# Which engines follow a hand-written table of times in a four-layer graph network: all five, or TensorE, VectorE and SyncE's queue alone

## The chip, the cores and the metric

The kernel runs on one core of one Trainium2 chip. The metric is device time in microseconds from the first to the last instruction of the program on that core; smaller is better. A core has five instruction streams that run side by side and wait for each other through semaphores: TensorE (PE, matrix products), VectorE (DVE), ScalarE (ACT), GpSimd (POOL) and SyncE (SP), which here only issues DMAs. Each stream runs strictly in its own order: an instruction that waits holds up everything behind it on its engine.

## The reference

64 independent graphs of 256 nodes with 512 features go through four layers. Each layer normalizes `x`, applies ReLU, runs a graph layer on the result and adds it to `x`. Cut to what matters:

```python
def _layernorm(x): return (x - mean) / sqrt(var + 1e-5)       # over the 512 features

# layer 0: q, k = split(h @ W_qk.T);  w = softmax(sum(q k^T / 8 * adj, -1), over nodes);  out = w * (h @ W_v.T)
# layer 1 (8 heads of 64):
feats = einsum('bnf,hfu->bhnu', X, W)
dense = leaky_relu(e_self[..., :, None] + e_neigh[..., None, :], 0.2)
dense = dense + NEG_BIG * (1.0 - A[:, None, :, :])
att = softmax(dense, axis=-1)
out = relu(einsum('bhij,bhju->bhiu', att, feats) + b)
# layer 2: Xp = X Wp + bp; attn = tanh(A * (Xp C^T) Xp^T) per head; out = relu(attn Xp)
# layer 3: q, k = split(h @ Wqk); w = sum(q * (adj @ (k * mask))) / sqrt(512); out = softmax(w) * (h @ Wv)
for each layer:
    h = maximum(_layernorm(x), 0)
    x = x + layer(h, adj)
```

## The kernel before

For each graph `b` the kernel defines some 150 small *steps* (a normalization, a product, a DMA). A table gives each step a time within its graph; a new graph starts every `PERIOD`, so five graphs are in work at once, each in another layer. The steps of all graphs are recorded in the order of these times. A scheduler then orders each engine's stream, but an engine in `PINNED` gets an edge from each of its instructions to the one recorded before it, so its stream is exactly the order of the table.

```python
PINNED = (mybir.EngineType.PE, mybir.EngineType.Activation, mybir.EngineType.DVE, mybir.EngineType.Pool, mybir.EngineType.SP,)

PERIOD = 60.2
TIMES = { ...
    "max2": 74.244, "ea1": 75.256, "max0": 75.757, "max3": 76.069, "ea3": 77.200, "ea0": 78.017, "max1": 78.219,
    "mxv": 78.317, "ea2": 80.651, "eg2": 82.397, "mxt": 85.102, "eg0": 86.489, "mr": 87.558, "eg1": 88.075, ...
    "eg3": 96.405, ...
    "yr": 197.444, "yv": 199.505, "yg": 201.580, "st3": 202.086, "rs3": 203.471, "pw3": 205.848, ... }
...
    def run(self, weights, graph, count):
        for _, b, name in self.sequence(count):
            ...
            graphs[b].steps[name]()
            for i in traced[n:]:
                if i.engine in PINNED:
                    if i.engine in self.last:
                        self.tc.add_manual_dep(i, self.last[i.engine], ... NoSync ..., reason="plan")
                    self.last[i.engine] = i.name
```

The steps that the text below follows, from three different layers, are these. Layer 1 (attention): `max` finds the largest masked score of each row, on VectorE; `ea`, `eg`, `eb`, `ex` make the attention weights of two heads, on four engines in turn; `po` is the product with the features.

```python
    def largest(i):                                   # max0..3: 16 instructions for a graph
        for h in range(i % 2 * 4, i % 2 * 4 + 4):
            nc.vector.tensor_tensor_reduce(junk, g["en"][:, h, :], g["adj"][:, c, :], 1.0, -BIG,
                                           OP.add, OP.max, g["mx"][:, c, h:h + 1])          # L851
    # mxv: four small VectorE instructions on mx (L861 to L865); mxt: a transpose of mx (L870)
    # mr, mb: DMAs of the result to DRAM and back to all partitions, as m

    def attention(p):                                 # p = 0..3, two heads each
        # ea{p}: four times
        nc.scalar.activation(e[:, s, j, :], g["es"][:, h, :], AF.Prelu, bias=..., alpha=0.2)   # L890
        # eg{p}:
        nc.gpsimd.tensor_tensor(e, e, g["negt"][:, None].to_broadcast([P, 2, NC, N]), OP.add)  # L897
        # eb{p}:
        nc.vector.tensor_tensor(e, e, g["m"][...], OP.subtract)                                # L903
        # ex{p}:
        nc.scalar.activation(g[f"e{p}"], g[f"e{p}"], AF.Exp)                                   # L909
        # po{p}: matmuls of e with feats (L921)
```

The end of layer 2 (`yg` on GpSimd and `yv` on VectorE add the layer's output to the two halves of `x`) and the start of layer 3 (normalization, `L662` to `L685`):

```python
        # yr: DMA sq_d -> hn (y)
        add_output(0, "yg", nc.gpsimd)      # L1076: xt[:, 0] += y[:, 0]
        add_output(1, "yv", nc.vector)      # L1076: xt[:, 1] += y[:, 1]
    # normed(layer): st: bn_stats, bn_aggr (L662, L664) | rs: var + eps (L669, VectorE)
    #   pw: power -0.5 (L673, GpSimd) | sh: -mean * rstd (L678, VectorE)
    #   hn: relu(x * rstd + shift), two halves (L685, ScalarE) | sq: transposes (L617) | sw, ht: DMAs
```

The end of layer 3, for the graph before that one, and the start of layer 0, for the graph after:

```python
    # zv1: row sums of q * aggregate (L1116, VectorE) -> wc
    # softp: TensorE spreads wc (L723) | softv: row maximum (L728, VectorE)
    # softa: exp on ScalarE (L733, L735) | softw, add: L740, L741, L747 on VectorE
    # qk0, qk1: projections on TensorE | qe0, qe1: copies of them to SBUF (L763, ScalarE)
    # score0: matmul that reads qk (L773, TensorE) | agg0, agg1: matmuls that read hn of layer 3 (L1095)
    # ga0, ga1: copies of agg (L1104, ScalarE) | xcv, xca: copies of xc (L995, ScalarE)
```

Of the kernel before, what the change touches and what calls it, by code (L numbers as in the profile page):

```python
# [31 lines left out]
NEG_BIG = -1e10  # L32
BIG = 3.0e38

PINNED = (mybir.EngineType.PE, mybir.EngineType.Activation, mybir.EngineType.DVE, mybir.EngineType.Pool, mybir.EngineType.SP,)

PERIOD = 60.2
TIMES = {
# [308 lines left out]
class Plan:  # L347
# [20 lines left out]
    def run(self, weights, graph, count):  # L368
        graphs = {-1: weights()}
        for _, b, name in self.sequence(count):  # L370
# [5 lines left out]
# [3 lines that stand above are left out]
# [783 lines left out]
```

## Time and profile before

| | |
|---|---|
| time, median of three runs | 3899.43 us (3897.83 to 3902.69) |
| profiled execution, span | 3884.0 us |
| granted TensorE clock, mean | 0.992 |
| ScalarE busy | 1668.5 us (43%) |
| DMA share of 16 engines | 60.8% |
| GpSimd L897 (`eg`), 256 of them | 601.8 us, 2371 ns each |
| GpSimd L1076 (`yg`), 64 of them | 108.2 us, 1691 ns each |
| VectorE L851 (`max`), 1024 of them | 446.3 us, 436 ns each |
| VectorE L678 (`sh`), 256 of them | 158.3 us, 618 ns each |

The span holds 64 graphs. In the middle of the run the same pattern comes back every 58.6 us: the `hn` of one layer starts at 1901.91 us and its successor at 1960.50 us. A span of 58.6 us of the timeline is therefore the unit in which everything below is counted. In a line of the timeline the first number is the start in us, the second the time from the first start to the last end of the merged instructions, then engine, line, operation, output and inputs, the count, and in brackets the idle time before and what ended it.

### The profile page before, as it was taken

How to read it: one execution, taken by the hardware profiler on the slowest of the kernel's cores; microseconds unless marked ns; L12 is line 12 of the kernel's file. 1: busy time of each engine (PE TensorE's matmuls, PEld its weight loads, DVE VectorE, ACT ScalarE, POOL GpSimd, SP SyncE). 2: the span in 40 equal slices, each digit the busy share in tenths (PEclk: the TensorE clock that was granted, in tenths of full speed). 3: DMA queues.
4: the chain of work that ended last, by engine and by line, in shares of the span. 5: the costliest groups of instructions: out<-in, count | busy, mean ns of one | idle time of the engine just before them, and what ended most of it. 6: DMA issues, size and time to landing. Idle time of an engine off the chain costs nothing.

```text
span 3884.0 us, 53839 instructions
## 1 busy us (share of the span) xinstructions
PE 3809.3 (98%) x17218; PEld 2443.6 (63%) x17218; DVE 3025.1 (78%) x7769; ACT 1668.5 (43%) x3205; POOL 1264.8 (33%) x1100
## 2 busy tenths in 40 slices
PE   7999999999999999999999999999999999999989
PEld 4756666666666666666666666666666666665564
DVE  6887888878877877877888778778777778776774
ACT  2443444444444444444444444444444444443342
POOL 1332333333333323323323323323323333333231
PEclk9999999999999999999999999999999999999989
DMA  7565666665665665666666666666666666665543
GB/s 211 177 190 170 188 189 185 192 194 176 199 196 174 200 195 177 197 194 180 193 190 188 191 190 188 188 189 189 187 188 191 186 190 191 185 190 163 173 149 107
DMA packets 921353, 717.64 MB, mean 185 GB/s; under 512 B 783792, under 2 KB 821232, under 8 KB 896496
## 3 DMA queue, kind: packets, MB, share of 16 engines
q1 hardware_dynamic: 921072, 714.21, 60.8%
q8 instruction: 138, 2.26, 0.2%
q14 instruction: 143, 1.17, 0.1%
HBM read 477.56 MB, written 236.45 MB: 184 GB/s over the span
## 4 chain that ended last, share of the span: by engine, by line
PE 88%; DVE 6%; DMA 3%; issue 1%; SPq 1%; ACT 0%; POOL 0%; DVEq 0%; POOLq 0%; ACTq 0%
PE bank L611 55%; PE bank L921 12%; PE bank L1009 6%; PE bank L1023 5%; PE bank L1095 5%; PE bank L987 3%; DVE junk L851 2%; PE bank L773 1%; DMA sq_d<-sq 1%; DVE sq L617 1%; PE bank L723 1%; DMA all<-m_d 1%; DMA all<-er_d 1%; DVE pair L903 1%; DMA ht<-sq_d 1%
## 5 line engine op out<-in xcount | busy, mean ns | idle before, releaser
L611 PE MATMUL bank<-w_s,ht 128*128 128x256 f32 (+2 forms) x3072 | 949.9, 462 | 14.8 <-DMA ht<-sq_d 9.5
L611 PE MATMUL bank<-wv_s,ht 128*128 128x512 f32 x2048 | 916.6, 595 | 0.0
L611 PEld LDWEIGHTS bank<-w_s,ht 128*128 128x128 f32 x3072 | 595.3, 197 | 352.3 <-issue 237.9
L611 PEld LDWEIGHTS bank<-wv_s,ht 128*128 128x128 f32 x2048 | 393.0, 197 | 415.4 <-issue 400.9
L897 POOL TENSOR_TENSOR pair<-pair,negt 128x1024 f32<-128x1024 f32 x256 | 601.8, 2371 | 51.5 <-ACT pair L890 47.3
L685 ACT ACTIVATE hn<-xt,shift,rstd 128x512 f32<-128x512 f32 x512 | 388.8, 806 | 433.1 <-DVE shift L678 424.4
L921 PEld LDWEIGHTS bank<-feats,pair 128*128 128x128 f32 x4096 | 512.2, 200 | 54.3 <-issue 29.6
L1048 ACT ACTIVATE pair<-pair 128x512 f32<-128x512 f32 x512 | 299.2, 625 | 558.4 <-DVE pair L1041 558.1
L921 PE MATMUL bank<-feats,pair 128*128 128x65 f32 x4096 | 507.5, 283 | 17.5 <-ACT pair L909 17.5
L890 ACT ACTIVATE pair<-all,ec 128x256 f32<-128x256 f32 x1024 | 417.1, 494 | 229.6 <-DMA all<-er_d 225.6
L851 DVE CUSTOM_DVE_ANT_0 junk<-all,adj 128x256 f32<-128x256 f32 x1024 | 446.3, 436 | 38.2 <-DMA all<-er_d 4.8
L611 PE MATMUL bank<-m_s,ht 128*128 128x512 f32 x1024 | 466.3, 599 | 1.9 <-DMA ht<-sq_d 1.2
L673 POOL TENSOR_TENSOR rstd<-rstd,power 128x2 f32<-128x2 f32 x256 | 180.2, 704 | 845.7 <-DVE rstd L669 715.7
L1041 DVE TENSOR_TENSOR pair<-bank,at 128x512 f32<-128x512 f32 x512 | 325.8, 679 | 109.6 <-PE bank L1009 108.7
L617 DVE STREAM_TRANSPOSE sq<-hn 128x512 f32<-128x512 f32 x512 | 338.5, 694 | 59.9 <-ACT hn L685 59.7
L1076 POOL TENSOR_TENSOR xt<-xt,hn 128x512 f32<-128x512 f32 x64 | 108.2, 1691 | 840.8 <-DMA hn<-sq_d 712.1
L903 DVE TENSOR_TENSOR pair<-pair,all 128x1024 f32<-128x1024 f32 x256 | 309.8, 1230 | 57.6 <-DMA all<-m_d 53.7
L662 DVE BATCH_NORM_STATS2 stats<-xt 128x6 f32<-128x512 f32 x512 | 327.2, 681 | 34.2 <-POOL xt L1076 27.5
L611 PEld LDWEIGHTS bank<-m_s,ht 128*128 128x128 f32 x1024 | 195.9, 196 | 208.4 <-issue 202.3
L946 POOL TENSOR_TENSOR xt<-xt,o 128x256 f32<-128x256 f32 x256 | 183.8, 728 | 409.1 <-DVE o L938 300.8
L909 ACT ACTIVATE pair<-pair 128x1024 f32<-128x1024 f32 x256 | 262.3, 1047 | 55.3 <-DVE pair L903 49.9
L1009 PE MATMUL bank<-xc,xpt 64*128 64x256 f32 x2048 | 256.7, 390 | 0.9 <-ACT xc L995 0.7
(74 smaller groups left out, 3793.2 us busy)
## 6 DMA issues: line engine op xcount, KB each, us to landing
sq_d<-sq SPq DMA_DIRECT2D x384, 512.0 KB
ht<-sq_d SPq DMA_DIRECT2D x1024, 128.0 KB
all<-er_d SPq DMA_DIRECT2D x128, 1024.0 KB
all<-m_d SPq DMA_DIRECT2D x64, 1024.0 KB
xt<-in_x_dram SPq DMA_DIRECT2D x64, 512.0 KB
xpt<-sq_d SPq DMA_DIRECT2D x256, 128.0 KB
hn<-sq_d SPq DMA_DIRECT2D x256, 128.0 KB
out_dram<-xt SPq DMA_DIRECT2D x64, 512.0 KB
```

Source lines behind the costliest of these rows:

```text
L611: nc.tensor.matmul(p, chunk(ht[:, k], c), w[:, k], start=(k == 0), stop=(k == KC - 1))
L617: nc.vector.transpose(sq.rearrange("p (r k i c) -> p c k r i", r=4, k=KC, c=NC)[:, c], t[:, c])
L662: nc.vector.bn_stats(stats[:, c, :], g["xt"][:, c, :])
L685: nc.scalar.activation(hn[:, c, :], g["xt"][:, c, :], AF.Relu, bias=st["shift"][:, c:c + 1], scale=st["rstd"][:, c:c + 1])
L851: nc.vector.tensor_tensor_reduce(junk, g["en"][:, h, :], g["adj"][:, c, :], 1.0, -BIG, OP.add, OP.max, g["mx"][:, c, h:h + 1])
L890: nc.scalar.activation(e[:, s, j, :], g["es"][:, h, :], AF.Prelu, bias=st["ec"][:, j, H + h:H + h + 1], alpha=0.2)
L897: nc.gpsimd.tensor_tensor(e, e, g["negt"][:, None].to_broadcast([P, 2, NC, N]), OP.add)
L903: nc.vector.tensor_tensor(e, e, g["m"][:, 2 * p:2 * p + 2, None, :].to_broadcast([P, 2, NC, N]), OP.subtract)
L921: nc.tensor.matmul(po[:, h % 4, :], chunk(e[:, s, j], i), feats[:, j, h, :], start=(j == 0), stop=(j == NC - 1))
L1009: nc.tensor.matmul(ps[s][:, m, :], chunk(g["xpt"][half, p], m), g["xc"][half, p, :], start=True, stop=True)
L1041: nc.vector.tensor_tensor(th[:, s], g[f"ps{p}{s}"].rearrange("p (m n) -> p m n", m=NC), g["at"], OP.mult)
L1048: nc.scalar.activation(g[f"th{p}"][:, s], g[f"th{p}"][:, s], AF.Tanh)
```

## The change

ScalarE and GpSimd are taken out of `PINNED`. Their data dependencies stay, and each is then ordered by the scheduler as it judges best; the other three streams stay tied to the table. The purpose is to let the two engines take whatever is ready, instead of standing before a step whose inputs the table expected earlier.

```diff
-PINNED = (mybir.EngineType.PE, mybir.EngineType.Activation, mybir.EngineType.DVE, mybir.EngineType.Pool, mybir.EngineType.SP,)
+PINNED = (mybir.EngineType.PE, mybir.EngineType.DVE, mybir.EngineType.SP,)
```

In the built programs, the streams of TensorE, VectorE and SyncE are the same instructions in the same order, with the same buffers. ScalarE and GpSimd have the same instructions in another order. In the middle of the run, GpSimd's order for one period is

```
before: am am, neg, negt, pw, yg, eg, pw, eg eg eg, pw, pa pa pa pa, pw
after:  neg, am am, negt, pw, eg eg eg eg, yg, pw, pw, pa pa pa pa, pw
```

and ScalarE's, from the copies `ye` on (`hn'` is one half of an `hn`, `softa` and `w` the two exponentials of a softmax):

```
before: ye ye hn, ea ea ea ea, qe qe hn, softa3 w3, softa0 w0, ex, ga0, ex ex, ga1, hn, ex, xcv xca, ta ta hn ta ta
after:  ye ye hn, ea ea ea ea, softa3, qe, hn', qe, hn', w3, ga0, ex, softa0 w0, ex, ga1, ex, xcv, hn, ex, xca, ta ta ta hn ta
```

(`ta`: the tanh of layer 2; neighbours such as `ex` and `ga` change places from one period to the next.)

## The prediction

> **What bounds the kernel now.** I read the page's first and second parts, then the waits of TensorE, then the timeline of one period, and last the same instructions early in the run, where the order of GpSimd was already once what the change makes of it.
>
> From the first part of the page, and from the waits of TensorE:
>
> ```profile
> PE 3809.3 (98%) x17218; PEld 2443.6 (63%) x17218; DVE 3025.1 (78%) x7769; ACT 1668.5 (43%) x3205; POOL 1264.8 (33%) x1100
> ...
> PE bank L921 <- ACT pair L909: 17.5, 7, 5.1
> ...
> PE bank L723 <- DVE bank L1116: 10.4, 4, 4.2
> ```
>
> TensorE is idle for 3884.0 - 3809.3 = 75 us in all. A busy share of pipelined matmuls alone proves little, but here the longest wait of TensorE for anyone adds up to 17.5 us in 7 times, and these lie in the filling and emptying of the pipeline of graphs. In the middle TensorE never waits. Two things follow. There is next to nothing to win: at most those 75 us, 2%, and most of them need the first and last graphs. And every microsecond by which TensorE is made to wait in a period of 58.6 us is paid in full, once for each graph. ScalarE (43%) and GpSimd (33%) have much idle time, so their order matters only through what they do to others.
>
> Now the timeline of one period, from the last `max` instructions to the first matmul of `score0`:
>
> ```profile
> 1918.03 6.49 ACT L890 ACTIVATE pair<-all,ec 128x256 f32<-128x256 f32 x16 [3.46 <-DMA all<-er_d]
> ...
> 1922.21 0.42 DVE L851 CUSTOM_DVE_ANT_0 junk<-all,adj 128x256 f32<-128x256 f32 x1
> ...
> 1923.31 0.17 DVE L865 TENSOR_TENSOR mx<-mx 128x16 f32<-128x16 f32 x1
> ...
> 1925.34 0.69 DVE L1076 TENSOR_TENSOR xt<-xt,hn 128x512 f32<-128x512 f32 x1 [1.86 <-DMA hn<-sq_d]
> 1925.44 1.72 POOL L1076 TENSOR_TENSOR xt<-xt,hn 128x512 f32<-128x512 f32 x1 [13.46 <-DMA hn<-sq_d]
> ...
> 1926.62 0.14 DVE L1116 DVE_READ_ACCUMULATOR bank<-bank,mask_c,cols 128x1 f32 x1
> ...
> 1927.12 2.35 POOL L897 TENSOR_TENSOR pair<-pair,negt 128x1024 f32<-128x1024 f32 x1
> ...
> 1929.06 0.14 PEld L723 LDWEIGHTS bank<-ident,wc 128*128 128x128 f32 x1 [0.23 <-issue]
> ...
> 1930.25 7.02 POOL L897 TENSOR_TENSOR pair<-pair,negt 128x1024 f32<-128x1024 f32 x3
> 1930.41 2.21 DVE L678 SCALAR_TENSOR_TENSOR shift<-mv,rstd 128x2 f32<-128x2 f32 x1
> ```
>
> The reader is to see four things. (1) GpSimd stands idle for 13.46 us before `yg`, while ScalarE has finished the first pair (four of the 16 L890) near 1919.7: the table makes `eg` wait behind `yg`. (2) Meanwhile VectorE runs the 16 `max` instructions undisturbed, 0.42 us each, one every 0.465 us, to 1922.63. (3) `zv1` ends at 1926.76 and TensorE takes its result at 1929.06, so it has 2.3 us to spare; over the steady periods this distance is 1.4 to 2.8 us, mostly 2.4. (4) Once `eg` runs, a VectorE instruction on 128x2 elements (L678) takes 2.21 us and ends when the running `eg` ends; in the 184 cases with no GpSimd instruction beside it the median is 0.15 us.
>
> The timeline of an early graph shows what happens when `eg` and `max` do meet:
>
> ```profile
> 214.99 0.43 DVE L851 CUSTOM_DVE_ANT_0 junk<-all,adj 128x256 f32<-128x256 f32 x1
> 215.02 7.60 POOL L897 TENSOR_TENSOR pair<-pair,negt 128x1024 f32<-128x1024 f32 x3 [5.51 <-ACT pair L890]
> ...
> 215.46 2.46 DVE L851 CUSTOM_DVE_ANT_0 junk<-all,adj 128x256 f32<-128x256 f32 x1
> ...
> 217.96 2.45 DVE L851 CUSTOM_DVE_ANT_0 junk<-all,adj 128x256 f32<-128x256 f32 x1
> ```
>
> They take turns: one `max` for each `eg`, start to start 217.96 - 215.46 = 2.50 us in place of 0.465.
>
> **What the Trainium skill says.** "SBUF — State Buffer", section "Who interferes with whom": a VectorE instruction with two SBUF inputs contends with a GpSimd instruction that reads SBUF, and the one that comes second is blocked for the whole instruction, not slowed. The trace agrees: L851 (`en` and `adj`, both in SBUF) 2.45 us, L678 2.21 us; while L1116, with one tensor in PSUM, has a median of 751 ns with and without GpSimd beside it. "TensorE: Matmul & The Clock Gate", section "Part 1: The HAM clock gate (the "warmup" mystery)": after an idle window of about 3.4 us TensorE's clock is halved, until a busy window has passed. The trace agrees: all idle gaps of TensorE over 3.2 us after its start are followed by a stretch at clock 0.50 of 3.4, 6.8 or 13.7 us, and there the 512-column matmuls start every 853 ns, against 429 ns elsewhere.
>
> **The change, part by part.** VectorE, TensorE and SyncE keep their order, so I move GpSimd's and ScalarE's instructions to the new order and keep every measured duration.
>
> *GpSimd: four `eg`, then `yg`* (57 graphs have exactly this order). The first `eg` can start near 1919.7. By then 10 of the 16 `max` have begun (1915.24 + 9 x 0.465 = 1919.4). The next four each wait for an `eg`: 4 x (2.50 - 0.465) = +8.1 us. The fifth waits for `yg`, which alone takes some 1.2 us (1.72 us minus the 0.5 us in which it stood behind `yv`): about +0.8 us. So the last `max` ends near 1922.6 + 8.9 = 1931.5, and `mxv`, four small instructions, near 1932.4. The data of `yv` came at 1925.3, so the idle 1.86 us before it is used up; `yv` and `zv1` follow at once, and `zv1` ends near 1932.4 + 0.1 + 1.4 = 1933.9 instead of 1926.8: +7.1 us. TensorE had 2.3 us to spare, so it waits 7.1 - 2.3 = 4.8 us before `softp3`.
>
> *TensorE's clock.* A gap of 4.8 us is longer than any window of 3.4 us needs. The nearest likeness in the trace is the single wait of 4.2 us for L1116 in the waits above: TensorE starts again at 3574.80 and the half clock lasts to 3579.75. Half of those 4.95 us is lost: 2.5 us.
>
> *What GpSimd gives back.* The later part of VectorE's work now runs without `eg` beside it: L678 takes 0.15 us in place of 2.21. This shortens VectorE's chain by 2 us, but behind `zv1`. It lets VectorE catch up with a TensorE that is now 7 us later, and wins no time for TensorE itself.
>
> *ScalarE.* `softa3` now stands before the copies `qe`, and half an `hn` between them. Counted from TensorE's new position, `softv3` ends some 2 us later than before (1932 on the old scale), `softa3` takes 0.6 us, `qe` and half an `hn` follow, and the second `qe` ends near 1933.8; `score0` needs it at 1934.6. It just fits. `xcv` before `hn` of layer 1 delays that `hn` by about 2.5 us and `ex3` behind it to about 1951, where `po3` wants it at 1950.5: at most 0.6 us, and the slower clock ahead of it covers that. I count 0 for ScalarE.
>
> Sum for a graph: 4.8 + 2.5 = 7.3 us. Times 57 graphs: 416 us. With 3899: 4315 us. For the first and last graphs, where the orders differ in other ways, I add nothing.
>
> **The rivals.** *Nothing happens* (same, 3870 to 3930): GpSimd and VectorE share little, and a stream with a third of its time busy has room. For it: the table's pattern was one choice among many, and `eg` finishes 8 us earlier. Against it: an earlier `eg` is of no use, since `eb` waits for the DMA of `m` until 1937.63 anyway, and the lock is plain in the trace. *No lock, only order* (4000 to 4080): if `eg` did not block `max`, `yg` would still end near 1930.9 instead of 1927.2, and `st3`, `pw3`, `hn` behind it would be 3.7 us later; `agg0` had 1.6 us in hand, so TensorE would wait 2 us for a graph, or 120 us. *Faster* (3820 to 3880): readiness order removes part of the 75 idle us at the ends. It would have to happen without the cost above. *Worse than the sum* (4450 to 4600): the half clock lasts for 13.7 us, as after two gaps in the trace, or `ex3` and `score0` add a second wait and with it a second drop of the clock.
>
> **Range and chances.** The wait of 4.8 us could be 3.5 to 6 (1.4 to 2.8 us in hand, and one `max` more or less caught), the clock's cost 1 to 4 us: 4.5 to 10 us for a graph at the extremes, 5 to 9.5 most likely, so 285 to 540 us: 4180 to 4440. Faster 0.02, same 0.05, slower 0.93.
>
> **What would show it.** In the profile after: L851 near 0.95 us on average in place of 436 ns ((11 x 0.42 + 4 x 2.45 + 1.25) / 16); L678 falls from 618 to about 160 ns; L1076 on GpSimd from 1691 to about 1250 ns. TensorE's wait "L723 <- DVE L1116" grows from 10.4 us to 57 x 4.8 = 270 us, and becomes the largest by far. The mean clock falls from 0.992 to about 0.95, with one drop in each period. I would be wrong if L851 keeps its 0.42 us (the lock is not met), if TensorE's largest wait is for ScalarE (L763, L909 or L685: the order of ScalarE is the cause), or if the clock stays at 0.99 (the sum loses 2.5 us for a graph).

## The result, and the profile after

The changed kernel takes 4309.38 us (4299.38 to 4315.26), against 3898.63 us before: 1.105 times the time, with an interval of 1.1026 to 1.1075. The predicted time was 4315 us.

The head and the first part of the page after. The busy time of an engine comes before its share of the span:

```profile
span 4310.0 us, 54091 instructions
...
PE 3959.5 (92%) x17218; PEld 2545.9 (59%) x17218; DVE 3418.9 (79%) x7769; ACT 1676.0 (39%) x3205; POOL 1282.9 (30%) x1100
```

The two longest waits of TensorE (us in all, times, longest):

```profile
PE bank L723 <- DVE bank L1116: 237.4, 56, 6.8
PE bank L921 <- ACT pair L909: 32.8, 58, 5.7
```

VectorE is busy for 394 us more with the same 7769 instructions: each of them has the same work, so the added time is time in which an instruction was held up, which the profile counts as busy. TensorE, too, is busy for 150 us more with the same matmuls: that is its clock, whose mean fell from 0.992 to 0.959. And it waits for L1116 (`zv1`) in 56 graphs, 4.2 us each.

The groups of L851, L1076 on GpSimd and L678 (busy us, then mean ns of one):

```profile
L851 DVE CUSTOM_DVE_ANT_0 junk<-all,adj 128x256 f32<-128x256 f32 x1024 | 947.3, 925 | 38.7 <-DMA all<-er_d 5.5
...
L1076 POOL TENSOR_TENSOR xt<-xt,hn 128x512 f32<-128x512 f32 x64 | 92.1, 1438 | 52.7 <-DMA hn<-sq_d 52.7
...
L678 DVE SCALAR_TENSOR_TENSOR shift<-mv,rstd 128x2 f32<-128x2 f32 x256 | 41.5, 162 | 82.5 <-POOL rstd L673 82.4
```

L851 costs 501 us more than before, L678 117 us less. The same stretch of one period as in the prediction, in the timeline after:

```profile
2002.00 6.49 ACT L890 ACTIVATE pair<-all,ec 128x256 f32<-128x256 f32 x16 [3.26 <-DMA all<-er_d]
...
2003.79 9.91 POOL L897 TENSOR_TENSOR pair<-pair,negt 128x1024 f32<-128x1024 f32 x4 [7.64 <-ACT pair L890]
2004.04 2.47 DVE L851 CUSTOM_DVE_ANT_0 junk<-all,adj 128x256 f32<-128x256 f32 x1
...
2006.55 2.46 DVE L851 CUSTOM_DVE_ANT_0 junk<-all,adj 128x256 f32<-128x256 f32 x1
...
2009.05 2.44 DVE L851 CUSTOM_DVE_ANT_0 junk<-all,adj 128x256 f32<-128x256 f32 x1
...
2011.54 2.44 DVE L851 CUSTOM_DVE_ANT_0 junk<-all,adj 128x256 f32<-128x256 f32 x1
...
2013.66 1.45 POOL L1076 TENSOR_TENSOR xt<-xt,hn 128x512 f32<-128x512 f32 x1
2014.02 1.36 DVE L851 CUSTOM_DVE_ANT_0 junk<-all,adj 128x256 f32<-128x256 f32 x1
2015.42 0.42 DVE L851 CUSTOM_DVE_ANT_0 junk<-all,adj 128x256 f32<-128x256 f32 x1
...
2017.30 0.75 DVE L1116 SCALAR_TENSOR_TENSOR bank<-bank,mask_c,cols 128x512 f32<-128x512 f32 x1
...
2018.17 0.48 PE L723 MATMUL bank<-ident,wc 128*128 128x128 f32 x1 [4.24 <-DVE bank L1116]
2018.44 3.26 PE L611 MATMUL bank<-wqk_s,ht 128*128 128x128 f32 x16
```

Four `max` wait behind an `eg` each, the fifth behind `yg`, the sixth is free; then `yv` and `zv1` follow without a pause, and TensorE has stood for 4.24 us. The last line shows the clock: the 16 matmuls of `qk` take 3.26 us. In the timeline before they took 2.05 us:

```profile
1929.71 2.05 PE L611 MATMUL bank<-wqk_s,ht 128*128 128x128 f32 x16
```

From the traces of all kernels I took the same chain, graph by graph, and averaged 40 graphs in the middle of the run. The stages follow each other without a gap or an overlap, so their sum is the period; us:

| stage | before | after | GpSimd free | ScalarE free |
|---|---|---|---|---|
| `er` ready to first `max` (a DMA) | 9.38 | 9.39 | 9.38 | 9.38 |
| the 16 `max` | 7.40 | 15.66 | 15.68 | 7.40 |
| last `max` to end of `zv1` | 4.16 | 3.10 | 3.09 | 4.19 |
| `zv1` to the matmul of `softp3` that reads it | 2.67 | 0.05 | 0.05 | 2.67 |
| `softp3` to `score0` on TensorE | 5.54 | 7.29 | 7.12 | 5.54 |
| `score0` to `xc` | 11.75 | 11.77 | 11.90 | 11.75 |
| `xc` to `fa` of the next graph | 13.09 | 13.80 | 13.09 | 13.74 |
| `fa` to `er` | 4.65 | 4.65 | 4.65 | 4.65 |
| period | 58.65 | 65.73 | 64.97 | 59.33 |

The loss of 7.08 us for a graph is in three places: 8.26 - 1.06 - 2.62 = 4.58 us by the blocked `max`, 1.75 us between `softp3` and `score0`, and 0.71 us between `xc` and `fa`.

### The profile page after: what moved, and what is told of

Same layout as the page of the kernel before. It is cut to its first block, busy times and chain, and to the rows that moved or that the text cites. A ratio compares the mean times of both kernels' runs of the same rounds, so it can differ in the third digit from the quotient of the medians.

```text
span 4310.0 us, 54091 instructions
## 1 busy us (share of the span) xinstructions
PE 3959.5 (92%) x17218; PEld 2545.9 (59%) x17218; DVE 3418.9 (79%) x7769; ACT 1676.0 (39%) x3205; POOL 1282.9 (30%) x1100
## 4 chain that ended last, share of the span: by engine, by line
PE 43%; DVE 38%; issue 9%; ACT 4%; DMA 3%; POOL 1%; SPq 1%; DVEq 0%; ACTq 0%; POOLq 0%
PE bank L611 23%; DVE junk L851 21%; PE bank L921 7%; PE bank L1009 6%; PE bank L1095 3%; DVE sq L617 3%; ACT hn L685 3%; DVE stats L662 2%; DVE bank L1116 2%; DVE pair L1041 1%; ACT pair L909 1%; PE bank L987 1%; DVE sq L1057 1%; DMA all<-er_d 1%; PE bank L1023 1%
## 5 line engine op out<-in xcount | busy, mean ns | idle before, releaser
L851 DVE CUSTOM_DVE_ANT_0 junk<-all,adj 128x256 f32<-128x256 f32 x1024 | 947.3, 925 | 38.7 <-DMA all<-er_d 5.5
L611 PE MATMUL bank<-wv_s,ht 128*128 128x512 f32 x2048 | 944.0, 609 | 5.1 <-DVE bank L1116 2.6
L897 POOL TENSOR_TENSOR pair<-pair,negt 128x1024 f32<-128x1024 f32 x256 | 634.4, 2507 | 527.0 <-ACT pair L890 498.9
L611 PEld LDWEIGHTS bank<-wv_s,ht 128*128 128x128 f32 x2048 | 406.4, 204 | 437.7 <-issue 417.3
L921 PEld LDWEIGHTS bank<-feats,pair 128*128 128x128 f32 x4096 | 521.0, 201 | 78.5 <-ACT pair L909 42.8
L921 PE MATMUL bank<-feats,pair 128*128 128x65 f32 x4096 | 523.8, 285 | 33.9 <-ACT pair L909 32.8
L903 DVE TENSOR_TENSOR pair<-pair,all 128x1024 f32<-128x1024 f32 x256 | 307.6, 1222 | 133.2 <-DMA all<-m_d 132.7
L909 ACT ACTIVATE pair<-pair 128x1024 f32<-128x1024 f32 x256 | 268.6, 1052 | 162.5 <-DVE pair L903 139.6
L733 ACT ACTIVATE bank<-bank,nmax 128x256 f32<-128x256 f32 x128 | 56.3, 440 | 692.2 <-DVE nmax L728 691.9
L723 PE MATMUL bank<-ident,wc 128*128 128x128 f32 x256 | 67.4, 310 | 242.1 <-DVE bank L1116 237.4
```

The lines of the kernel that those rows point to most:

```text
L611: nc.tensor.matmul(p, chunk(ht[:, k], c), w[:, k], start=(k == 0), stop=(k == KC - 1))
L903: nc.vector.tensor_tensor(e, e, g["m"][:, 2 * p:2 * p + 2, None, :].to_broadcast([P, 2, NC, N]), OP.subtract)
L921: nc.tensor.matmul(po[:, h % 4, :], chunk(e[:, s, j], i), feats[:, j, h, :], start=(j == 0), stop=(j == NC - 1))
```

## The experiments

My theory was the one of the prediction: `eg` on GpSimd and `max` on VectorE block each other, TensorE waits, its clock falls, and ScalarE's order is free of cost. The rivals were that only the lateness of `yg` counts, that ScalarE's order is a part of it, and that the clock's fall is covered by something else.

### One engine at a time

**pool_free**: only GpSimd is untied. **act_free**: only ScalarE is.

```diff
-PINNED = (mybir.EngineType.PE, mybir.EngineType.DVE, mybir.EngineType.SP,)
+PINNED = (mybir.EngineType.PE, mybir.EngineType.Activation, mybir.EngineType.DVE, mybir.EngineType.SP,)   # pool_free
+PINNED = (mybir.EngineType.PE, mybir.EngineType.DVE, mybir.EngineType.Pool, mybir.EngineType.SP,)          # act_free
```

> GpSimd alone is untied, ScalarE stays tied. Theory (GpSimd's four eg before yg meet the max instructions of VectorE, and TensorE waits for zv1): the whole loss is here, 4310 us (4280 to 4340), L851 near 925 ns on average, TensorE's wait L723 for L1116 near 240 us, clock 0.96. Rival (ScalarE's order is a part of the loss): 4000 to 4250.

Measured: 4266.61 us, 1.0945 (1.0928 to 1.0961) times before. L851 904 ns, TensorE's wait for `zv1` 240.2 us. The signs are those of the theory, but the time lies 13 us under its range and 17 us over the rival's: most of the loss, not all of it.

> ScalarE alone is untied, GpSimd stays tied. Theory: no loss, 3900 us (3880 to 3930), L851 at 436 ns, clock 0.99. Rival (ScalarE's order costs something: softa3 ahead of qe, or xcv ahead of the hn of layer 1): TensorE waits for L763 or L909 in each period, 3950 to 4150.

Measured: 3941.74 us, 1.011 (1.0095 to 1.0125). L851 433 ns. Against before in the same runs (3896.51 us) GpSimd costs 370 us and ScalarE 45 us; together 415, and the change cost 411. GpSimd is nine tenths of the loss, but my 0 for ScalarE was wrong, and the rival's 3950 us was too much. The timeline of this kernel shows where; the bracket in the last line is TensorE's wait:

```profile
1972.81 1.22 DVE L903 TENSOR_TENSOR pair<-pair,all 128x1024 f32<-128x1024 f32 x1
...
1975.16 0.59 ACT L995 COPY xc<-bank 128x512 f32<-128x512 f32 x1 [3.03 <-PE bank L987]
1975.64 1.52 ACT L685 ACTIVATE hn<-xt,shift,rstd 128x512 f32<-128x512 f32 x2
...
1977.06 1.04 ACT L909 ACTIVATE pair<-pair 128x1024 f32<-128x1024 f32 x1
...
1978.16 2.10 PE L921 MATMUL bank<-feats,pair 128*128 128x65 f32 x16 [0.35 <-ACT pair L909]
```

ScalarE stands for 3.03 us before `xcv`, although the input of the `hn` behind it (shift, 1972.73 + 0.16 us) is long there; `ex3` comes last, and `po3` waits for it.

**scalar_hn_first**: as act_free, but `hn` of layer 1 and `xcv` keep the table's order.

```diff
+                if name in ("hn1", "xcv") and i.engine == mybir.EngineType.Activation:
+                    (an edge from the last such instruction to this one)
```

> GpSimd tied, ScalarE free but for one chain: the hn of layer 1 and xcv in the order of the table, which puts hn and ex3 ahead of xcv again. Theory (ScalarE's part of the loss, 3942 us against 3897, is po3 waiting for ex3 behind xcv and hn): TensorE's wait L921 for L909 returns to some 17 us, 3907 us (3893 to 3922). Rival (softa3 ahead of qe, or the ends of the run, cost as much): 3930 to 3945 us.

Measured: 3915.65 us, 1.004 (1.0028 to 1.0051). The wait of L921 for L909 falls from 37.2 us in 58 times to 22.9 us in 11, and the period from 59.33 to 58.84 us. So that one exchange is most of ScalarE's part, 28 of 45 us, each counted against before in the same runs (3898.76 us here). Of the 17 us that stay, 11 are in the middle (the period is 0.19 us over that of before, times 57) and the rest in the first and last graphs; what they wait for I did not follow up.

### What on GpSimd it is

**three_edges**: as the changed kernel, but `yg`, `pw3` and the `eg` are chained on GpSimd in the table's order. All else on both engines is free.

```diff
+                if i.engine == mybir.EngineType.Pool and (name in ("yg", "pw3") or name[:2] == "eg"):
+                    (an edge from the last such instruction to this one)
```

> As the changed kernel, but on GpSimd yg, pw3 and the eg are tied to each other in the order of the table (yg, eg, pw3, eg eg eg); all else on GpSimd and ScalarE stays free. Theory: the relation of these three alone is the cause, 3900 us (3880 to 3930). Rival (the other moves, neg before am and the free ScalarE, cost too): 3950 to 4200.

Measured: 3949.33 us, 1.0132 (1.0117 to 1.0147). That is 19 us over my range, because ScalarE is free here too, and act_free within 8 us. So the order of these six instructions is GpSimd's whole part; `neg` before `am` costs nothing to speak of.

**yg_first**: one edge only, each `eg` behind the last `yg`; the scheduler then puts `yg`, four `eg`, `pw3`.

```diff
+                    if name == "yg":
+                        self.yg = i.name
+                    if name[:2] == "eg" and self.yg:
+                        (an edge from yg to this one)
```

> As the changed kernel, but with one edge: each eg stands behind the last yg. The scheduler now puts yg, then all four eg, then pw3. Theory: the max instructions are undisturbed (L851 at 0.42 us), but pw3 stands behind four eg until about 1937 us on the scale of the timeline before, so L678, hn of layer 3 and with it the second qe are some 5 us late; TensorE now waits about 3.5 us for L763 or L685 in each period, with a drop of the clock behind it: 4120 to 4290 us, near 4230. Rival (only the meeting of eg and max matters): 3900 us.

Measured: 4219.77 us, 1.0832 (1.0806 to 1.0857). The two largest waits of TensorE, and then the group of L851:

```profile
PE bank L773 <- ACT qk L763: 180.7, 59, 5.1
PE bank L921 <- ACT pair L909: 33.0, 59, 6.0
```

```profile
L851 DVE CUSTOM_DVE_ANT_0 junk<-all,adj 128x256 f32<-128x256 f32 x1024 | 479.2, 468 | 37.5 <-DMA all<-er_d 4.5
```

The blocking is gone, and four fifths of the loss, 328 of 411 us, are back under another name: `pw3`, a 0.7 us instruction, stands behind some 9.3 us of `eg`, VectorE's `sh3` waits for it (L678 idle 422.4 us before it, against 63.3 before), then `hn`, then the second `qe`, then `score0`. In the table's order one `eg` fits exactly between `yg` and `pw3`: in the timeline before it runs from 1927.12 to 1929.47 us, and VectorE's `rs3`, whose result `pw3` takes, ends at 1929.50 us.

**yg_on_vector**: as the changed kernel, but both halves of the addition are on VectorE.

```diff
-        add_output(0, "yg", nc.gpsimd)
+        add_output(0, "yg", nc.vector)
```

> As the changed kernel, but both halves of the addition of layer 2's output are on VectorE, so no yg stands behind the four eg on GpSimd. Theory (eg blocks max): the wait for zv1 stays, since four max still wait for four eg; the fifth is free (0.8 us less) and VectorE has 0.7 us more to do before zv1: 4300 us (4270 to 4340). Rival (the late yg is the cause, by st3 and pw3 behind it): 3900 to 3980 us.

Measured: 4264.01 us, 1.0945 (1.0917 to 1.0974). With no `yg` on GpSimd at all, the loss stays; TensorE waits for L1116 for 185.3 us in 57 times, L851 takes 883 ns. So `yg` on GpSimd is not the cause. (The wait is 3.3 us, where I expected about that of the changed kernel, 4.2: the time is 36 us under my figure and 6 us under my range.) `pw3` still stands behind four `eg` here; the next kernel leaves it there and takes away the blocking.

**eg_writes_only**: as the changed kernel, GpSimd in the same order, but `eg` writes zeros and reads nothing. It leaves out the scores and the mask of layer 1.

```diff
-                nc.gpsimd.tensor_tensor(e, e, g["negt"][:, None].to_broadcast([P, 2, NC, N]), OP.add)
+                for _ in range(2):
+                    nc.gpsimd.memset(e[:, :, :, :], 0.0)
```

> As the changed kernel and with GpSimd in the same order, but eg is two memsets of the pair to zero instead of the addition of the mask: GpSimd still holds about 2 us for each eg, but reads nothing of SBUF. (It leaves out the mask and the scores of layer 1.) Theory (the loss is the blocking of VectorE's two-input max by a GpSimd instruction that reads SBUF): L851 stays at 0.42 us, no wait for zv1, 3890 to 3960 us; a little may be left because yg ends some 2 us later than before. Rival (only the late place of yg in the order costs, or any GpSimd instruction blocks VectorE): 4150 to 4310 us, and in the second case L851 still near 0.9 us.

Measured: 3976.41 us, 1.0209 (1.0189 to 1.023). The groups of both:

```profile
L897 POOL MEMSET pair<- 128x1024 f32 x512 | 477.4, 954 | 539.4 <-ACT pair L890 524.8
...
L851 DVE CUSTOM_DVE_ANT_0 junk<-all,adj 128x256 f32<-128x256 f32 x1024 | 434.2, 424 | 37.8 <-DMA all<-er_d 4.6
```

GpSimd works for 1.91 us in the place of each `eg`, in the same stretch and ahead of the same `max`, and no `max` is slowed: 424 ns, and the train of 16 lasts 7.40 us as before. So a GpSimd that is busy and writes does not block `max`; it is the reading. This is what the Trainium skill says ("SBUF — State Buffer", section "Who interferes with whom": contention with a GpSimd instruction that reads SBUF, not with one that only writes it), here with both numbers. The time is 35 us over act_free, though, and 16 us over my range: TensorE waits more for `ex` (51.7 us against 37.2). `yg` ends later here, at 2022.6 us with the first `ea` at 2011.9, 10.7 us after it, where before it was 9.1; whether that alone is the 35 us I did not try. The clock has a part in it: between 300 us after the start and 350 us before the end it falls 17 times, 14 of them at L921, against 4 times in act_free.

### Whether the clock's fall can be won back

The clock in stretches of the changed kernel, after the gap and later (the columns are busy us of PE, PEld, DVE, ACT and POOL with counts, then the clock, the DMA share and GB/s):

```profile
2018.20:2021.00 2.80, 2.80 (x13) 2.80 (x14) 2.46 (x9) 0.46 (x2) 0.70 (x1) 0.50 0.00 0
2021.20:2025.00 3.80, 3.80 (x14) 1.94 (x13) 3.70 (x5) 1.86 (x5) 0.00 (x0) 1.00 0.37 101
```

The kernels of this part give TensorE useless work in the gap before `softp3`, in the bank that `softp3` then overwrites; only the number differs (**filler** 7, **filler_4** 4, **filler_2** 2).

```diff
                 pr = g.take("bank", name="pr")
+                for _ in range(7 if layer == 3 else 0):
+                    nc.tensor.matmul(pr, ident, wv[:, 0, :], start=True, stop=True)
```

> As the changed kernel, but TensorE does seven 512-column matmuls into the bank of softp3 just before softp3, in each graph; their results are overwritten. That is 7 x 0.43 = 3.0 us of useless work in a gap of 4.25 us. Theory (half of the loss beyond the wait is the halved clock after a gap of over 3.4 us): the gap shrinks to some 1.3 us, the clock stays at 0.99, and the kernel with more work is faster than the changed one: 4140 to 4190 us. Rival (the wait alone counts, the clock's record costs nothing): 4310 us, as TensorE waits for the same zv1; or, if the filler is not hidden, 4480.

Measured: 4344.77 us, 1.1151 (1.1123 to 1.1179). The size was wrong: each product stands in the trace as two matmuls of 0.43 us, so the filler took 6.0 us, longer than the gap. In the middle it still gave a little: `softp3` to `score0` is back at 5.54 us, but `softp3` now comes 1.49 us after `zv1` instead of 0.05, and the period is 65.47 us against 65.73.

> The filler again in a size that fits: the trace of the filler of seven shows that each 512-column product in float32 is two matmuls of 0.43 us, so seven took 6.0 us, longer than the gap. Four take 3.4 us and leave some 0.8 us of the gap of 4.25 us. Theory (the halved clock after a gap costs about 2 us for a graph): no drop in the middle of the run, the filler hidden, so the changed kernel less 57 x 2 us: 4190 us (4160 to 4230), clock near 0.985. Rival (the half clock costs nothing that is not hidden): 4310 us.

Measured: 4329.92 us, 1.1105 (1.1072 to 1.1139).

> Two products, 1.7 us, which leave a gap of about 2.5 us, less than the 3.4 us of a clock window. Theory (the drop needs a gap of over about 3.2 us): the same time as with four, 4190 us (4160 to 4230), with TensorE's wait at L723 three times as long. Rival (any gap in each period lowers the clock): between that and 4310 us, with drops in each period.

Measured: 4311.64 us, 1.1062 (1.1025 to 1.1099). Both miss, and none is faster than the changed kernel (4309.38 us); filler_2 is where its rival put it. By stages, filler_4 did what it was for: `softp3` to `score0` takes 5.62 us, as good as before (5.54), against 7.29. But `xc` to `fa` grew from 13.80 to 14.98 us, and there the clock now fell (22 of the 27 falls in periods 5 to 56, numbered from 0 by the graph whose `max` runs, start in L921 or L1009), so the period is 65.50 us. In the first and last graphs, where there is no gap, the filler also stands unhidden.

**filler_gpsimd**: four fillers again, on pool_free, where `po3` does not wait for `ex3`, and in graphs 5 to 57 alone.

> The kernel with GpSimd alone untied (4267 us, and without the wait of po3 for ex3), with four filler products before softp3 in graphs 5 to 57 alone, so that none stands unhidden at the ends of the run. In the runs of the fillers the stretch from softp3 to score0 fell from 7.3 us to 5.6, so the clock's cost there went away, but the clock now fell later, in L921 and L1009, where po3 waits for ex3. Theory (the clock's cost is real and can be won back where no other gap follows): no drops in the middle, 1.6 us less for a graph, 53 x 1.6 = 85 us: 4180 us (4165 to 4210). Rival (VectorE, late in every period, sets the period whatever TensorE's clock is, and the clock's cost is covered by its lateness): new waits of TensorE for L909, L685 or L747 take the place of the clock's cost, 4240 to 4270 us.

Measured: 4364.5 us, 1.1221 (1.1195 to 1.1248): 95 us over the upper end of the rival's range, so both miss, though the sign that the rival named, a new wait for L909, is there. Three lines of TensorE's timeline; the last two show it:

```profile
2021.96 0.32 PE L723 MATMUL bank<-ident,wc 128*128 128x128 f32 x1 [0.91 <-DVE bank L1116]
2036.12 2.10 PE L921 MATMUL bank<-feats,pair 128*128 128x65 f32 x16 [0.36 <-ACT pair L909]
2038.70 3.67 PE L921 MATMUL bank<-feats,pair 128*128 128x65 f32 x16 [0.47 <-ACT pair L909]
```

TensorE arrives at `po` sooner and now waits for `ex` there, twice, for half a microsecond. And the second `po` takes 3.67 us where the first takes 2.10: in periods 5 to 56 the clock falls 39 times in L921, for 6.8 us mostly. `ex` is late because VectorE's first `eb` (L903) waits 3.63 us for the DMA of `m`, which starts from `mxt`, behind the blocked `max`.

**filler_no_m**: the same kernel, but `eb` subtracts a resident tile of zeros in place of `m`, so it does not wait for that DMA. It leaves out the subtraction of the row maximum.

```diff
-                nc.vector.tensor_tensor(e, e, g["m"][:, 2 * p:2 * p + 2, None, :].to_broadcast([P, 2, NC, N]), OP.subtract)
+                nc.vector.tensor_tensor(e, e, b1_bc.rearrange("p (s n) -> p s n", s=2)[:, :, None, :]
+                                        .to_broadcast([P, 2, NC, N]), OP.subtract)
```

> As the last kernel (GpSimd untied, filler of four), but eb subtracts a bias of zeros that lies in SBUF in place of m, the row maximum that comes back by DMA; the softmax keeps its value, and VectorE no longer waits for the DMA of m (3.6 us before the first L903 in the last kernel's timeline). It leaves out the subtraction of the maximum. Theory (right behind the clock's cost lies a second wait: mxt, late by the blocked max, makes m, eb, ex and po late, and the small gaps in L921 lower the clock once more): the gaps in L921 go, the clock stays full in the middle, and the time falls to what the filler should have given: 4180 us (4150 to 4215). Rival (VectorE is late by itself, not for the DMA of m, or the clock falls in L921 anyway): 4260 to 4365 us.

Measured: 4184.19 us, 1.0747 (1.0718 to 1.0776), where theory said 4180. TensorE's waits:

```profile
PE bank L723 <- DVE bank L1116: 61.0, 55, 6.7
PE bank L611 <- DMA ht<-sq_d: 16.0, 13, 6.3
```

L921 is out of the first places, the clock is at 0.988, and the period is 63.72 us against 67.00 of the same kernel with `m`. So with the filler, the wait by way of `m` costs 180 us, with the falls of the clock behind it. Against pool_free (4266.61 us), which has `m` and no filler, the gain is 82 us, and this is not divided further: a kernel without `m` and without filler was not run. In pool_free TensorE's waits for L909 come to 20.6 us in 17 times, so I would expect little from `m` alone.

## Why the prediction was right, and where it was not

**The bound, and the cost of a wait in every period**: right. TensorE had nothing to give, and what it waited came out in full.

**The blocked `max`**: right, and with the right size. I said +8.1 us by four `eg` and +0.8 by `yg`, 8.9 us; the train grew by 8.26 us. I said that `zv1` would come 7.1 us later, and it came 7.20 later (8.26 - 1.06). I said 4.8 us of waiting for `softp3`; the stages give a delay of 4.58, and the wait in the trace is 4.2 (237.4 us in all, where I had said 270). L851 was to have 0.95 us on average, and has 0.925, though my bracket gives 15.67 / 16 = 0.98: that is a period with four blocked `max`, and with seven graphs of 64 at the old 0.436 it comes to 0.92; L678 160 ns, and has 162; L1076 on GpSimd 1250 ns, and has 1438, since it still stands behind one `max`. eg_writes_only and yg_on_vector show the mechanism against its rivals, and three_edges shows that the order of `yg`, `eg` and `pw3` is all of GpSimd's part.

**The clock**: the fall is there in every period, but the term was too large, 2.5 us against 1.75, because the half clock mostly lasted 3.4 us and not the 5 us of my one likeness. And the reasoning was wrong in one point. I added the clock's cost as if nothing lay behind it, and wrote that VectorE would "catch up with a TensorE that is now 7 us later". The fillers show that VectorE does not have that time in hand: in filler_4 the clock is restored behind `softp3`, yet the period falls by 0.23 us and not by 1.75, because the late `mxt` returns through `m`, `eb`, `ex` and `po`, and the clock falls there. The one filler kernel that is faster than its like without filler is the one without `m` (filler_no_m). That the 1.75 us and this wait lie over each other fits these runs; without the run that leaves out `m` alone it is not shown in full.

**ScalarE**: wrong in size. The step "at most 0.6 us, and the slower clock ahead of it covers that. I count 0" had the right place (`xcv` and `hn` before `ex3`, `po3` waiting) and the right 0.6 us, and then cancelled it. It is 0.71 us for a graph in the changed kernel: my reading, which no run tests alone, is that `ex3` is late with VectorE, so that the slower clock ahead of it gives TensorE's `po3` no room. `softa3` ahead of `qe` cost nothing in the middle, as said.

**The sum** came out at 7.3 us against 7.08 because a clock term too large by 0.75 and a ScalarE term too small by 0.71 cancel; that the total is so close is luck. 57 x 7.08 = 404 us of the 411 measured; the first and last graphs add little.

**The rivals**: "No lock, only order" falls with eg_writes_only, where `yg` and `pw3` are late and the blocking is gone (3976 us), though yg_first shows that order alone can cost 328 us, at another place than I had named.

## What to carry to other kernels

Two engines that block each other, as VectorE and GpSimd do here, are coupled without any semaphore that shows it. A hand-made order may hold them apart without saying so, and a scheduler that takes whatever is ready brings them together; look for one short instruction whose time is sometimes that of its neighbour's. In a pipeline whose bound engine is full, an earlier start elsewhere is worth nothing, and a freed engine should first be asked what it will now run beside. And before you count on winning back one wait, look at what is late behind it: the same late engine often reaches the bound engine by a second way.

## What the runs showed of the hardware beyond that

- The clock of TensorE does not need a gap of over 3.2 us to fall. In yg_first gaps of 2.6 to 2.9 us bring falls in some periods and not in others; in filler_2 gaps of about 2.5 us do in 28 of 53; in filler_gpsimd gaps of about 0.5 us between the 65-column matmuls of L921 do (39 falls in periods 5 to 56), while those of 0.35 us before `po3` in act_free, 50 in all, had two falls behind them in the middle of the run. The Trainium skill ("TensorE: Matmul & The Clock Gate", section "Part 1: The HAM clock gate (the "warmup" mystery)") speaks of an idle window of about 3.4 us; here the measurement decides, and a window that is only in part idle is enough.
- Much of the rule can be read from the traces. In each of the 14 the clock changes only at points of a fixed grid of 3.413 us (to within 7 ns). I laid this grid over the middle of every run (from 300 us after the start to 350 us before the end) and took the windows at full clock of which L921 takes less than 5%: all 222 in which TensorE was busy for under 40% were followed by half clock, none of the 10661 with 60% or more was, and 27 of 137 in between were. By this a gap of 4.24 us always makes a fall, since even when split evenly it leaves a window busy for (3.413 - 2.12) / 3.413 = 38%, and in the changed kernel each of the periods 10 to 49 has one; a gap of 2.5 us does so only where it lies mostly in one window. With more of L921 in the window falls came at up to 90% busy; by which rule, these runs don't tell.
- A memset on GpSimd did not slow VectorE's `max`, which has two inputs in SBUF: in eg_writes_only L851 has a median of 424 ns with it and without it. It did hold up a VectorE instruction with one input: L863 (a `tensor_scalar` on 128x16 of `mxv`) takes 628 ns as the median of the 60 that met a memset, and 174 ns in the 3 that met nothing on GpSimd. `zv1` had the 0.45 us to spare.
